# Spreading the softmax reciprocals over the heads' partitions: a matrix product with diagonal blocks, or a trip through memory

## The chip, the cores and the metric

One core of a Trainium2 chip runs the whole layer in one launch. The metric is device time in microseconds; several runs are made and their median is compared. A profiled execution of the same kernel gives the trace that all durations below come from.

## The reference, cut to what matters

Three blocks follow each other on x (4 batches, 256 tokens, width 256): cross-attention to a context of 4096 rows per batch, a layer that sends a quarter of the tokens to self-attention and the rest to a selective scan (ssm), and a mixture of 8 experts of which each token uses 2. The change lies in the cross-attention alone:

```python
q1 = split_heads(x1 @ Wq1, N1)                     # 8 heads of 64
k = jnp.concatenate([k1, k2], axis=1)              # 256 own keys and 4096 context keys
v = jnp.concatenate([v1, v2], axis=1)
sim = jnp.einsum('bihd,bjhd->bhij', q1, k) * scale
attn = jax.nn.softmax(sim, axis=-1)
out = jnp.einsum('bhij,bjhd->bihd', attn, v)
return out.reshape(B, N1, h * d) @ Wo + bo
```

The kernel divides by the softmax sum after the product with v: each row of `out` is multiplied with the reciprocal of its sum of exponentials.

## The kernel before, in words

**Groups and steps.** The cross-attention takes two heads at a time: 4 batches times 4 pairs are 16 groups, G = 0 to 15. A group has 8 steps s, each of 32 queries against all 4352 keys, so the loop runs over n = 8G + s, and two more steps drain it. In a step `scores(n)` makes the scores in PSUM (su), `copy_max` (L1299) brings them to SBUF and takes maxima, `stat` (L1311, L1316) joins the maxima, `exps` (L1327) makes exponentials and their sums ls for the step before, and `turn` (L1336) transposes them. A step is 128 partitions: 4 quarters of the keys times 32 queries.

**What fills a step.** The rest of TensorE's time in a step goes to `pieces`: at s = 0, 6 and 7 keys of the next group (`k_chunk`, psk, L1226, copied by ACT at L1214), at s = 2, 3 and 4 values of this group (`v_chunk`, psv, L1263, copied at L1267), and at s = 1 and 5 `values(m)`: 136 products po (L1345) that multiply the exponentials of four steps with v. One po holds 64 dimensions of each of two heads on the partitions and 128 queries along the free axis; `values_out` (L1382) copies it to ao.

**The sums.** After a group's last exponentials, at s = 0 of the next group, `sums(G-1)` adds the four quarters' sums with a product (psl, L1359) and takes reciprocals (rl, L1364): they lie as 2 heads x 32 queries on 64 partitions, 8 steps along the free axis. The normalisation wants them the other way: queries along the free axis, the same value on all 64 partitions of a head. Before, DVE multiplies rl with diagonal blocks (dg, 64 x 256, L1366), and at s = 1, between the first and second piece of po, `spread` multiplies dg with a constant of ones per head (pair) on TensorE: psr, 128 x 256, in PSUM (L1373). `normalize` (L1388) multiplies ao with it, one half in the middle of step s = 1 and one at its end.

**Queues, banks and order.** The order of all instructions is written out by hand (`manual_schedule`). Side work (router, small attention, ssm scan of the batch before) is made of generators that `slot` lets run one piece at a time, by a planned time `now` to which each piece adds its cost. Three PSUM banks with the tag "m" (`bank`, and the tiles psk, psv, po) serve all of these in turn; a tile waits until the earlier tile in its bank has been read. In-order engines: what waits, holds back all behind it. The SP queue issues nearly all loads: the context chunks ctx (512 KB each, `load_ctx`, L1130; four buffers, so that SP runs ahead by four), weights, and in the scans bb and cb (L615), spread copies of the ssm's B and C, which POOL uses at L637 and L650. The pieces of side work that are named below run for batches 0, 1 and 2 beside the groups of the next batch (the first of them at G = 4, 8 and 12): pspr (L553), its copy projT (L557), psas (L419), psdt (L579) and its readers delta and ev (L586), psat (L437), pa (L427, L428); at a scan's end zs (L764) and pssd (L769); after the last group psx (L1392) and the experts.

Of the kernel before, what the change touches and what calls it, by code (L numbers as in the profile page):

```python
# [8 lines left out]
F32 = mybir.dt.float32  # L9
AF = mybir.ActivationFunctionType  # L10
ALU = mybir.AluOpType
# [3 lines left out]
P = 128  # L15
B, T, D = 4, 256, 256
# [3 lines left out]
H, HD = 8, 64  # L20
# [17 lines left out]
def bc(ap, axis, n):  # L38

    ap = ap.unsqueeze(axis)  # L40
    shape = list(ap.shape)
    shape[axis] = n
    return ap.to_broadcast(shape)
# [3 lines left out]
def perceiver_layer(ctx: ExitStack, tc: tile.TileContext, a: dict, out: bass.AP):  # L47
    nc = tc.nc
# [5 lines left out]
    dram = ctx.enter_context(tc.tile_pool(name="dram", bufs=2, space=bass.MemoryType.DRAM))  # L54
    fin = ctx.enter_context(tc.tile_pool(name="fin", bufs=1))
# [166 lines left out]
    def bank(name):  # L222
        return ps_m.tile([P, 512], F32, tag="m", name=name)
# [831 lines left out]
    now = [0.0]  # L1055
    active = []

    def start(g):
        active.append([g, now[0], 0.0])
# [6 lines left out]
    def slot(budget):  # L1066

        room[0] = budget
        for item in list(active):
            if item[1] <= now[0] and item[2] <= room[0]:  # L1070
                room[0] -= item[2]
                step(item)

    def step(item):
        r = next(item[0], None)
        if r is None:
            active.remove(item)
        else:
            item[1:] = now[0] + r[0], r[1]
# [23 lines left out]
    with ExitStack() as s1:  # L1103
# [17 lines left out]
        def load_self(G):  # L1121
            return load_weights(G, ("wk1", "wq1"), "wself", 1)
# [26 lines left out]
        def load_later():  # L1149
# [11 lines left out]
        dm = same[:, 0, :]  # L1161
        nc.vector.tensor_reduce(
            out=dm, in_=ident.rearrange("p (c i) -> p i c", c=4), axis=AX.X, op=ALU.add
        )
        for q in range(1, 4):
            nc.vector.tensor_copy(same[:, q, :], dm)
        quarter = fin.tile([P, 4, 2], F32, name="quarter")
        nc.vector.tensor_reduce(
            out=quarter[:, :, 0], in_=ident.rearrange("p (c i) -> p c i", c=4), axis=AX.X,
# [17 lines left out]
        def turn_x(b):  # L1187
# [9 lines left out]

        su = ps_s.tile([P, 5 * 512], F32, name="su")


        pair = fin.tile([2 * 32, P], F32, name="pair")
        nc.vector.tensor_copy(
            pair.rearrange("p (j d) -> p j d", j=2), bc(quarter[: 2 * 32, 0:2, 0], 2, HD)
        )
        qzs = [fin.tile([P, 2, T], F32, name=f"qz{i}") for i in range(2)]
        for t in qzs:
            nc.gpsimd.memset(t, 0.0)
# [11 lines left out]
        def k_chunk(G, g):  # L1219
            b = G // NHP  # L1220
            if G not in kts:
                kts[G] = wk.tile([P, 4, QK], F32, tag="kt", name="kt")
            ct = load_ctx(b, g)
            ps = ps_m.tile([P, 512], F32, tag="m", name="psk")
            for c in range(KD):
                nc.tensor.matmul(  # L1226
                    ps, wqk[G][:, 0, c, :], ct[:, c, :],
                    start=(c == 0), stop=(c == KD - 1),
                )
            keys_out(G, g * (CK // 4), ps)  # L1230
# [118 lines left out]
                        start=(k == 0), stop=(k == NJ - 1),  # L1349
                    )  # L1350

        dgs, rss = {}, {}

        def sums(G):

            b, hp = divmod(G, NHP)
            ps = bank("psl")
            for j in range(2):
                nc.tensor.matmul(  # L1359
                    ps[j * 32 : (j + 1) * 32, :8], dm, lss[b][:, hp, :, j],  # L1360
                    start=True, stop=True,
                )
            rl = fin.tile([2 * 32, 8], F32, tag="rl", name="rl")
            nc.vector.reciprocal(rl, ps[: 2 * 32, :8])  # L1364
            dgs[G] = fin.tile([2 * 32, 8, 32], F32, tag="dg", name="dg")
            nc.vector.tensor_tensor(  # L1366
                dgs[G], bc(rl, 2, 32), bc(dm[: 2 * 32, :], 1, 8), ALU.mult
            )

        def spread(G):  # L1370

            rss[G] = bank("psr")[:, :T]
            nc.tensor.matmul(  # L1373
                rss[G], pair, dgs[G].rearrange("p s i -> p (s i)"), start=True, stop=True
            )

        def values_out(m):
# [39 lines left out]
        with tc.manual_schedule():  # L1417
            norms = {}
            k_chunk(0, 0)
            wself[0] = load_self(0)  # L1420
            nc.scalar.dma_start(out=bo_bc, in_=a["xbo"].partition_broadcast(P))
            for _ in norm(0):
                pass
            for g in range(1, NCH):
                k_chunk(0, g)
                if g == 4:
                    turn_x(0)
            k_self(0)
            start(load_later())
            wv[0] = load_v(0)  # L1430
            N = 8 * NG
            for n in range(N + 2):
                G, s = divmod(n, 8)
                new, old = n < N, 1 <= n <= N


                pieces, took = [], 1.75
                if s == 5 and G + 1 < NG:
                    wv[G + 1] = load_v(G + 1)
                if s % 4 == 1:  # L1440
                    m, took = n // 4 - 1, 1.95
                    if m >= 0:
                        pieces = [
                            lambda i=i: values(m, i, min(i + 9, NJ)) for i in range(0, NJ, 9)
                        ]
                elif 2 <= s <= 4 and G < NG:
                    pieces = [
                        lambda g=g: v_chunk(G, g) for g in range(3 * s - 6, 3 * s - 3)
                    ]
                elif G + 1 < NG:  # L1450
                    if s == 0:
                        wqk[G + 1] = load_qk(G + 1)
                        wself[G + 1] = load_self(G + 1)
                    pieces = {
                        0: [lambda g=g: k_chunk(G + 1, g) for g in range(3)],
                        6: [lambda g=g: k_chunk(G + 1, g) for g in range(3, 6)],
                        7: [lambda: k_self(G + 1)]
                        + [lambda g=g: k_chunk(G + 1, g) for g in range(6, 8)],
                    }[s]


                tail = n >= N - 2

                def piece(i):
                    if i < len(pieces):
                        pieces[i]()
                    if i < len(pieces) or tail:
                        now[0] += took

                if new:  # L1470
                    scores(n)
                    now[0] += 2.1
                if old:
                    exps(n - 1)
                if new:
                    copy_max(n)
                piece(0)
                if s % 4 != 1:
                    slot(1.3)
                    piece(1)  # L1480
                    if old:
                        turn(n - 1, 0)
                    if new:
                        stat(n)
                        now[0] += 0.3
                    if s == 0 and n:
                        sums(G - 1)
                        now[0] += 0.2
                    if old:
                        turn(n - 1, 1)  # L1490
                    slot(1.3 if tail else 0.5)
                    piece(2)
                    slot(2.9)
                else:
                    last = s == 1 and G
                    if last:
                        spread(G - 1)
                        now[0] += 0.6
                    slot(1.5)
                    piece(1)  # L1500
                    if new:
                        stat(n)
                        now[0] += 0.3
                    slot(2.8)
                    if last:
                        normalize(m - 1)
                    if n == N + 1:

                        psx[B - 1] = bank("psx")
                        project(B - 1, 0, psx[B - 1], range(NHP))  # L1510
                        add(B - 1, 0, psx[B - 1])
                        project(B - 1, 1, psx[B - 1], range(NHP - 1))
                    piece(2)
                    slot(1.5)
                    piece(3)
                    if n > 4:
                        values_out(m)
                    if old:
                        turn(n - 1, 0)
                        turn(n - 1, 1)  # L1520
                    if last:
                        normalize(m)
                        if m % 8 == 7:
                            start_first(finish_batch(m // 8))
                b = n // 32 + 1
                if b < B:
                    if n % 32 == 20:
                        norms[b] = norm(b)
                    if n % 32 in (20, 22):
                        next(norms[b])  # L1530
                    if n % 32 == 29:
                        turn_x(b)
# [299 lines left out]
```

## Time and profile before

| | |
|---|---|
| median of 3 runs | 1555.44 us (1549.75 to 1558.04) |
| profiled execution | 1555.58 us, of which the span 1553.9 us |
| mean granted TensorE clock | 0.977 |
| TensorE (PE) busy | 1461.9 us, 94% |
| VectorE (DVE) busy | 1057.1 us, 68% |
| ScalarE (ACT) busy | 758.9 us, 49% |
| GpSimd (POOL) busy | 412.0 us, 27% |
| DMA | 223.41 MB, 144 GB/s mean |
| psr: 32 passes (16 products) | 376 to 793 ns each |
| dg: 16 instructions | 416 to 757 ns each |

The span is the time from the first to the last instruction in the profile. A line of the timeline has the start in us, the length in us of a run of like instructions, the engine (SPq and ACTq are DMA issues), the source line, the operation, what it writes and reads, shapes, how many, and in brackets the idle time of the engine before it with what ended that. PEld is the loading of weights, beside PE. Each matrix product in f32 stands as two passes.

### The profile page before, as it was taken

To read this page: it belongs to the slowest core of one execution; us is meant where nothing else is said; L and a number is where in the kernel's file an instruction comes from. 1 tells how busy PE (TensorE), PEld (TensorE's weight loads), DVE (VectorE), ACT (ScalarE), POOL (GpSimd) and SP (SyncE) were. 2 spreads that over 40 slices of the span, in tenths; PEclk is the share of its full clock that TensorE was granted. 3 is DMA by queue.
4 is the path that set the end of the run, shared out by engine and by line. 5 is a ranking of instruction groups with operands and counts; after the bars stand their busy time and mean duration, and the time that the engine had idled before them with its cause. 6 is when DMAs were issued, how large, how long until landed. Compare 5 with 4: busy or idle time off the path is not lost.

```text
span 1553.9 us, 37283 instructions
## 1 busy us (share of the span) xinstructions
PE 1461.9 (94%) x15686; PEld 1039.5 (67%) x15686; DVE 1057.1 (68%) x1812; ACT 758.9 (49%) x1486; POOL 412.0 (27%) x464
## 2 busy tenths in 40 slices
PE   7999999999999999999999999999998868988799
PEld 3757667576667475766665767757665558778587
DVE  1666666666699976565999866658988633499453
ACT  3444454454666644555667454546664413534211
POOL 1000000000089940000799500005996011110100
PEclk9999999999999999999999999999999968999899
DMA  7445543524344525243454343334543115777471
GB/s 240 149 131 160 161 139 107 180 72 143 120 147 140 182 83 192 79 145 100 141 176 158 113 144 126 99 112 162 159 127 114 42 55 183 253 250 259 125 233 48
DMA packets 157767, 223.41 MB, mean 144 GB/s; under 512 B 14976, under 2 KB 76160, under 8 KB 157600
## 3 DMA queue, kind: packets, MB, share of 16 engines
q1 hardware_dynamic: 152368, 211.45, 42.7%
q10 hardware_dynamic: 3744, 5.51, 1.1%
q0 software_dynamic: 1488, 4.07, 0.9%
q8 instruction: 124, 2.03, 0.5%
q14 instruction: 43, 0.35, 0.1%
HBM read 216.56 MB, written 4.42 MB: 142 GB/s over the span
## 4 chain that ended last, share of the span: by engine, by line
PE 63%; POOL 14%; DVE 13%; issue 4%; ACT 3%; DMA 2%; ACTq 0%; SPq 0%; DVEq 0%; POOLq 0%
PE po L1345 12%; PE su L1279 11%; PE psv L1263 11%; PE psk L1226 9%; POOL y L652 5%; POOL db L637 5%; POOL db L650 4%; DVE sp L1299 4%; PE su L1287 2%; PE pg L1749 2%; PE pu L1749 2%; PE pde L1762 2%; DVE pt L1336 2%; DVE db L739 1%; DVE db L644 1%
## 5 line engine op out<-in xcount | busy, mean ns | idle before, releaser
L1299 DVE TENSOR_SCALAR_CACHE_REDUCE sp<-su 128x1088 f32<-128x1088 f32 x256 | 318.8, 1281 | 182.0 <-PE su L1287 182.0
L1336 DVE STREAM_TRANSPOSE pt<-sp 128x1088 f32<-128x1088 f32 x256 | 328.0, 1295 | 57.0 <-PE po L1345 56.9
L1327 ACT ACTIVATE sp<-sp,nb 128x1088 f32<-128x1088 f32 x256 | 305.2, 1195 | 13.9 <-DVE nb L1316 13.7
L1345 PE MATMUL po<-pt,v 128*64 128x128 f32 x4352 | 263.9, 278 | 2.3 <-DVE pt L1336 1.3
L1279 PE MATMUL su<-kt,qz 64*32 64x512 f32 x4096 | 256.0, 609 | 4.4 <-DVE nb L1316 3.7
L1226 PE MATMUL psk<-ctx,wk 128*128 128x512 f32 x512 | 245.1, 612 | 10.2 <-DMA ctx<-in_ctxT 7.7
L1345 PEld LDWEIGHTS po<-pt,v 128*64 128x64 f32 x4352 | 241.7, 139 | 14.1 <-issue 7.7
L1263 PE MATMUL psv<-wv,ctx 128*128 128x128 f32 x2048 | 250.3, 279 | 0.6 <-DMA ctx<-in_ctxT 0.3
L1263 PEld LDWEIGHTS psv<-wv,ctx 128*128 128x128 f32 x2048 | 236.1, 192 | 6.7 <-issue 1.4
L1226 PEld LDWEIGHTS psk<-ctx,wk 128*128 128x128 f32 x512 | 91.4, 191 | 94.3 <-issue 85.0
L1214 ACT COPY kt<-psk 128x512 f32<-128x512 f32 x128 | 74.8, 585 | 158.6 <-PE psk L1226 158.4
L1279 PEld LDWEIGHTS su<-kt,qz 64*32 64x32 f32 x4096 | 63.3, 108 | 124.4 <-issue 93.0
L652 POOL TENSOR_TENSOR y<-y,db 128x192 f32<-128x192 f32 x192 | 135.2, 704 | 15.1
L1267 ACT COPY v<-psv 128x512 f32<-128x512 f32 x144 | 79.2, 558 | 119.8 <-PE psv L1263 118.5
L644 DVE TENSOR_TENSOR_SCAN db<-da,db 128x384 f32<-128x384 f32 x96 | 123.2, 1284 | 14.4 <-POOL db L637 3.7
L650 POOL TENSOR_TENSOR db<-db,cb 128x384 f32<-128x384 f32 x96 | 110.8, 1154 | 26.4 <-DVE da L642 26.4
L395 POOL TENSOR_TENSOR kbd<-qk,hmask 128x512 f32<-128x512 f32 x8 | 8.2, 1045 | 407.1 <-ACT qk L385 407.1
L637 POOL TENSOR_TENSOR db<-bb,xc 128x384 f32<-128x384 f32 x96 | 111.2, 1181 | 0.2
L1287 PEld LDWEIGHTS su<-kt,qz 128*32 128x32 f32 x2048 | 34.6, 109 | 109.3 <-issue 109.3
L632 ACT ACTIVATE da<-delta,A_log_sb 128x192 f32<-128x192 f32 x192 | 75.4, 447 | 51.1 <-DVE da L642 38.4
L1382 ACT COPY ao<-po 128x128 f32<-128x128 f32 x32 | 8.5, 264 | 152.5 <-PE po L1345 152.5
L1311 PEld LDWEIGHTS su<-mq,same 128*128 128x128 f32 x256 | 41.1, 191 | 54.7 <-DVE mq L1306 37.8
(278 smaller groups left out, 1587.2 us busy)
## 6 DMA issues: line engine op xcount, KB each, us to landing
ctx<-in_ctxT SPq DMA_DIRECT2D x256, 512.0 KB, 4.8
gateT<-in_gateT SPq DMA_DIRECT2D x27, 512.0 KB, 4.0
upT<-in_upT SPq DMA_DIRECT2D x27, 512.0 KB, 5.1
downT<-in_downT SPq DMA_DIRECT2D x27, 512.0 KB, 6.2
bb<-bcd SPq DMA_DIRECT2D x24, 192.0 KB, 4.3
cb<-bcd SPq DMA_DIRECT2D x24, 192.0 KB, 3.6
wv<-in_wv SPq DMA_DIRECT2D x32, 128.0 KB, 2.4
in_w<-in_in_w SPq DMA_DIRECT2D x32, 128.0 KB, 3.8
```

What stands on the lines that cost most here:

```text
L637: nc.gpsimd.tensor_tensor(db, bbs[k], bc(xc[:, m, :], 1, SG), ALU.mult)
L644: nc.vector.tensor_tensor_scan(out=db, data0=da, data1=db, initial=0.0, op0=ALU.mult, op1=ALU.add,)
L650: nc.gpsimd.tensor_tensor(db, db, cbs[k], ALU.mult)
L652: nc.gpsimd.tensor_tensor(y[:, m, :], y[:, m, :], db[:, s, :], ALU.add)
L1226: nc.tensor.matmul(ps, wqk[G][:, 0, c, :], ct[:, c, :], start=(c == 0), stop=(c == KD - 1),)
L1263: nc.tensor.matmul(ps[:, i * P : (i + 1) * P], lhsT, wv[G][:, w, c, :], start=(c == 0), stop=(c == KD - 1),)
L1267: nc.scalar.copy(v.rearrange("p k d -> p (k d)"), ps[:, : n * P])
L1279: nc.tensor.matmul(su[q * 32 : (q + 1) * 32, SC[j] + lo : SC[j] + lo + 512], qT[r, j, s * 32 : (s + 1) * 32], kt[r, q, lo : lo + 512], sta ...
L1299: nc.vector.tensor_scalar(out=sps[n][j], in0=su[:, SU[j] : SU[j] + QK], scalar1=1.0, scalar2=None, op0=ALU.mult, op1=ALU.max, accum_out=nm ...
L1327: nc.scalar.activation(sps[n][j], sps[n][j], AF.Exp, bias=nbs[n][:, j : j + 1], accum_out=lss[b][:, hp, s, j : j + 1],)
L1336: nc.vector.transpose(pts[m, j][:, i, :], sps[n][j])
L1345: nc.tensor.matmul(pos[m][j * HD : (j + 1) * HD, :], vts[m // 2, k // 4][:, k % 4, j * HD : (j + 1) * HD], pts[m, j][:, :, kk * 32 : (kk + ...
```

## The change

The diagonal blocks, the constant of ones and the product go. `spread` now lies at s = 0, right after the third piece and before the last `slot`, and holds three DMAs: two on ACT's queue, one for each head, that write the 32 x 8 reciprocals into memory with queries contiguous, and one on SP's queue that reads each head's 256 values into all of its 64 partitions (rs in SBUF, 128 x 256). `normalize` reads rs. The 0.6 us that the plan added for the product is gone too.

```diff
-        pair = fin.tile([2 * 32, P], F32, name="pair")
-        nc.vector.tensor_copy(
-            pair.rearrange("p (j d) -> p j d", j=2), bc(quarter[: 2 * 32, 0:2, 0], 2, HD)
-        )
...
-        dgs, rss = {}, {}
+        rls, rss = {}, {}
...
-            rl = fin.tile([2 * 32, 8], F32, tag="rl", name="rl")
-            nc.vector.reciprocal(rl, ps[: 2 * 32, :8])
-            dgs[G] = fin.tile([2 * 32, 8, 32], F32, tag="dg", name="dg")
-            nc.vector.tensor_tensor(
-                dgs[G], bc(rl, 2, 32), bc(dm[: 2 * 32, :], 1, 8), ALU.mult
-            )
+            rls[G] = fin.tile([2 * 32, 8], F32, tag="rl", name="rl")
+            nc.vector.reciprocal(rls[G], ps[: 2 * 32, :8])
 
         def spread(G):
 
-            rss[G] = bank("psr")[:, :T]
-            nc.tensor.matmul(
-                rss[G], pair, dgs[G].rearrange("p s i -> p (s i)"), start=True, stop=True
+            rd = dram.tile([2, 8, 32], F32, tag="rd", name="rd")
+            for j in range(2):
+                nc.scalar.dma_start(
+                    out=rd[j].rearrange("s i -> i s"), in_=rls[G][j * 32 : (j + 1) * 32, :]
+                )
+            rss[G] = fin.tile([P, T], F32, tag="rs", name="rs")
+            nc.sync.dma_start(
+                out=rss[G],
+                in_=rd.rearrange("j s i -> j (s i)").unsqueeze(1).to_broadcast([2, HD, T]),
             )
...
                     slot(1.3 if tail else 0.5)
                     piece(2)
+                    if s == 0 and n:
+                        spread(G - 1)
                     slot(2.9)
                 else:
                     last = s == 1 and G
-                    if last:
-                        spread(G - 1)
-                        now[0] += 0.6
                     slot(1.5)
```

## The prediction

> **What bounds the kernel now.** I read the page first: engine shares, slices, chain.
>
> ```profile
> PE 1461.9 (94%) x15686; PEld 1039.5 (67%) x15686; DVE 1057.1 (68%) x1812; ACT 758.9 (49%) x1486; POOL 412.0 (27%) x464
> ...
> PE po L1345 12%; PE su L1279 11%; PE psv L1263 11%; PE psk L1226 9%; POOL y L652 5%; POOL db L637 5%; POOL db L650 4%; DVE sp L1299 4%; PE su L1287 2%; PE pg L1749 2%; PE pu L1749 2%; PE pde L1762 2%; DVE pt L1336 2%; DVE db L739 1%; DVE db L644 1%
> ```
>
> TensorE carries the attention stage; in three stretches (about 440-555, 765-870 and 1075-1190 us) the chain runs through POOL and DVE, the selective scan. Next the busy time by stretch: one without side work, one inside a scan.
>
> ```profile
> 228.00:262.00 34.00, 34.00 (x433) 22.89 (x432) 20.72 (x35) 14.50 (x26) 0.00 (x0) 1.00 0.50 157
> ...
> 780.00:805.00 25.00, 25.00 (x324) 17.46 (x317) 24.27 (x39) 15.34 (x32) 22.77 (x26) 1.00 0.47 121
> ```
>
> The columns are length, PE, PEld, DVE, ACT, POOL, clock, DMA share, GB/s. Without side work PE has no gap, so what leaves PE shortens the kernel; in a scan DVE and POOL are full. Then the timeline around one product with the diagonal blocks (G=0):
>
> ```profile
> 98.00 0.45 SPq L1130 DMA_DIRECT2D ctx<-in_ctxT  x1
> ...
> 99.09 0.20 DVE L1364 RECIPROCAL rl<-psl 64x8 f32<-64x8 f32 x1
> 99.33 0.42 DVE L1366 TENSOR_TENSOR dg<-rl,same 64x256 f32<-64x256 f32 x1
> ...
> 103.10 2.19 PE L1345 MATMUL po<-pt,v 128*64 128x128 f32 x36
> ...
> 105.22 0.70 PE L1373 MATMUL psr<-dg,pair 64*128 64x256 f32 x2
> ...
> 105.84 2.19 PE L1345 MATMUL po<-pt,v 128*64 128x128 f32 x36
> ...
> 108.47 0.28 DVE L1388 TENSOR_TENSOR ao<-ao,psr 128x128 f32<-128x128 f32 x1
> ```
>
> Nine microseconds lie between the reciprocal and its first use, and DVE's next instruction starts only at 112.09: that is the room for a trip through memory. Last, PE's timeline for G=4, where side work shares the three PSUM banks:
>
> ```profile
> 399.06 1.08 PE L419 MATMUL psas<-kbd,qk 128*64 128x512 f32 x4 [0.49 <-ACT projT L557]
> ...
> 407.67 0.66 PE L437 MATMUL psat<-ident,pa 128*128 128x128 f32 x4 [1.45 <-ACT ev L586]
> ```
>
> psas does not read projT and psat does not read ev: PE waits for a bank to be emptied, while psr holds another.
>
> **What the Trainium skill says.** (1) "DMA: Bandwidth & Descriptors", section "Why a DMA increments its semaphore by 16 and not by 1": a DMA runs on the largest k up to 16 that divides the outermost sizes of both sides. The new read's source is [2, 64 repeats, 256], so k=2; no DMA of before shows that. (2) The same page, "Rules for kernel authors": a last dimension that isn't contiguous becomes one descriptor per element. The trace agrees: behind the 512-element column load dt_b lies a burst of 544 packets, nearly all of 4 bytes (9 ns each), in 1.1 us. (3) The same page, "Two DMAs through the same engine are not ordered": the issuer must wait for the first DMA's semaphore; in the built program the read on SP waits for both writes. (4) "Perfetto Trace Analysis", "Optimization Strategy": consistent bubbles can mean too little PSUM; the 0.49 and 1.45 us above, there at G=4, 8 and 12, agree.
>
> **Removed, PE.** In the 64 po matmuls that start at 108.28 and take 3.71 us they follow each other every (3.71-0.28)/63 = 0.0545 us. From 103.10 to 105.84 are 2.74 us; 36 matmuls need 1.96; so a psr pair with its two changes of shape takes 0.78. At G=0 to 3, 7 and 11 PE has no other limit: 6 x 0.78 = 4.7 us. At G=4, 8, 12 psr is followed by pspr, where one change of shape (0.2, the step into psr) remains: 3 x 0.58 = 1.7. At G=15 PE runs at half clock (1.50 us from the po before to the po after, less a step of 0.1) and the tail waits for it: 1.4.
>
> **Removed, a PSUM bank.** Comparing the two built programs with their waits: instructions keep their order on every engine, only the psr, dg and pair instructions are gone; psat now waits for the first psdt's ev, two reads earlier, psas for a kt copy that is long done, psdt for pa. So 0.49+1.45 = 1.94 us go at each of G=4, 8, 12: 5.8 us. What is late next is psat's own input pa, done by 402.3, ahead of 405. The planner's lost 0.6 us per group moves nothing.
>
> **Removed, DVE.** Sixteen dg of 0.42 us; beside free DVE time they are worth nothing. At G=5, 9, 13 dg takes 0.76 and is in the chain: 3 x 0.7 = 2.1 us. The normalising product reads SBUF instead of PSUM: 32 x 0.25, between 0.1 less and 0.1 more each, 0 taken, since it lies in idle DVE time.
>
> **Added: the trip.** Per group two issues on ACT, one on SP. ACT: 0.34-0.48 us per issue in the trace, so 0.9 us ahead of the next exps (or da); those feed transposes over 6 us later (101.45 to 112.09): nothing. At G=14 ACT reaches the issue 2.75 us before the reciprocal (1171.95, 1174.70), with the da's of a scan behind it that starts at 1182.5: nothing. The issues stand behind the last kt copy, which ends 2.3 us after the reciprocal (1.8 in scan stretches). Writes of 256 4-byte elements: lower end 1.4 us (bcd, 24 KB out to memory), upper end 6.9 (a column load behind other traffic); I take 2.0, as the queue on ACT is empty. The second lands 4.75 us after the reciprocal. SP then issues the read: first packet 1.0 us later (bcd: 0.85), 64 packets of 1 KB on each of two engines at 46 ns (median of such packets) = 2.95, 0.6 to report: 4.5 us. Lower end 2.4 (wv, the same 128 KB on all engines); upper end 8.6, with 110 ns per packet, near the 104 mean of the broadcast bb and cb. rs is there 9.3 us after the reciprocal; DVE can wait until 12.4 without side work (11.8 at G=6, 10, 14): hidden, with 2.5 to 3.1 to spare.
>
> **Added: SP waits, and what is queued behind.** SP holds the read from its turn until the writes land, and in order behind it stand four ctx loads (at G=2 they were issued at 229.4, 233.5, 235.3 and 237.5) that now start about 241. On the two engines the first ctx follows the read: 5.75+2.95 = 8.7, plus 16 packets of 2 KB at 84 ns = 1.35, plus 0.6 = 10.7 us after the reciprocal. The first psv needs it at 14.9 less 0.8 = 14.1: 3.4 spare (2.5 at G=5, 9, 13, where cb and bb stand between). Hidden, but at G=0, where constants stand between (5.3 us of issues in before), I charge 1.0. At G=6 and 10 a cb load (531.44) now starts at about 546.5 and lands at 551.5, while the product that needs it (L650) starts at 549.62 and POOL is the chain: 2 us late, half of it regained because POOL then runs beside less DVE work; the saved 0.8 is lost and 0.6 more: -1.2 for both. At G=14 the delayed cb lands about when it is needed (1182.35): +0.5 kept.
> Tail, G=15: no copy ahead on ACT; rs at 1255.55+0.9+1.8+4.5 = 1262.8, psx needs it at 1265: hidden.
>
> **Sum.** 4.7+1.7+1.4+5.8+2.1+0.5-1.2-1.0 = 14.0 us. The profiled execution took 1555.58 us (span 1553.9, 1.7 around it), 0.1 from the runs' median of 1555.44: 1541.5 us.
>
> **Rivals.** (A) Forecast: gain 8 to 20 us. (B) The gain is swallowed: PE's savings before a scan's end are lost where zs waits for POOL, and bank waits are replaced by psat's or psdt's data. For it: about a third of the chain near the scans is POOL and DVE; against: G=4 has no other late input. Without the 5.8 and with cb 3 us late twice: 14-5.8-4 = 4, 1551. (C) Slower: the SP hold. If writes take 3.6 us (the quickest column loads of 1 KB and more) and the read 8.6, the chain is 5.7 late; the first psv then waits 5.7-3.1 = 2.6 us on average at 13 groups, 34 us against 14 gained: 1575. It decides from about 3 us over my estimate and costs 13 us per us beyond; at 4.1 over it cancels the gain. For it: nothing in before shows two-engine reads or 4-byte writes to memory; against: packet costs are measured and both rings are empty then. (D) The freed bank removes further waits in psv and the trip is quicker than thought: gain over 20, about 1532.
>
> **Chances.** A 0.60, B 0.17, C 0.14, D 0.09. Half a per cent is 7.8 us, about what a measurement here tells from no change. Faster: A, D and 0.02 of B = 0.71; same 0.15; slower 0.14. The range leaves out C's most (above) and D's better half: 1534 to 1557.
>
> **What would show it.** po groups 1.96 us apart with nothing between; psas and psat without waits; rs landing in 4 to 5 us from issue, ahead of ao; ctx issued in a burst some 5 us after rl; psv without a wait on DMA ctx; POOL L650 idle on cb about 2 us at two groups. Wrong if psv or ao wait for DMAs at most groups, or if rs takes over 8 us.

## The result, and the profile after

The changed kernel takes 1591.83 us (median of 4 runs, 1589.5 to 1593.62) where the kernel before took 1555.76 on the same chip: ratio 1.0239, 95% interval 1.0222 to 1.0256. It is 36 us slower; the forecast was 14 us faster. The span of its profiled execution is 1591.8 us, the mean granted clock 0.971.

The page after, engines and chain, as the first two lines of before were read:

```profile
PE 1465.2 (92%) x15654; PEld 1046.4 (66%) x15654; DVE 1054.1 (66%) x1795; ACT 759.7 (48%) x1486; POOL 397.5 (25%) x464
...
PE su L1274 9%; PE psk L1221 9%; PE psv L1258 9%; PE po L1340 8%; DVE sp L1294 5%; POOL y L652 4%; POOL db L650 4%; DVE db L644 3%; POOL db L637 3%; DVE pt L1331 2%; DMA rs<-rd 2%; DMA rd<-rl 2%; DMA ctx<-in_ctxT 2%; PE pg L1747 2%; PE su L1282 2%
```

TensorE's share fell from 94% to 92% although the product is gone, and three DMAs stand in the chain that were not there: the write of the reciprocals (rd<-rl), the read (rs<-rd), and the context loads. A stretch without side work, 34 us long as in the prediction (columns: stretch, length, PE, PEld, DVE, ACT, POOL, clock, DMA share, GB/s):

```profile
232.00:266.00 34.00, 31.81 (x383) 20.93 (x376) 19.84 (x33) 14.86 (x27) 2.30 (x3) 1.00 0.42 137
```

PE had no gap in such a stretch before; now it stands for 2.2 us at full clock. The timeline around the first trip (G=0; start, length, engine, line, operation, shapes, and in brackets the idle time before it with what ended that) shows where:

```profile
98.26 0.20 DVE L1359 RECIPROCAL rl<-psl 64x8 f32<-64x8 f32 x1
...
100.20 0.85 ACTq L1367 DMA_DIRECT2D rd<-rl  x2
102.27 4.15 PE L1340 MATMUL po<-pt,v 128*64 128x128 f32 x72
...
106.83 3.71 PE L1340 MATMUL po<-pt,v 128*64 128x128 f32 x64
...
107.28 0.66 SPq L1371 DMA_DIRECT2D rs<-rd  x1
...
111.36 0.73 SPq L1130 DMA_DIRECT2D ctx<-in_ctxT  x1
...
112.20 0.29 DVE L1387 TENSOR_TENSOR ao<-ao,rs 128x128 f32<-128x128 f32 x1 [5.10 <-DMA rs<-rd]
...
115.66 2.66 PE L1258 MATMUL psv<-wv,ctx 128*128 128x128 f32 x12 [2.88 <-DMA ctx<-in_ctxT]
```

The writes are issued at 100.20 and SP, which waits until both have landed, issues the read at 107.28: 7.1 us, where 2.0 was priced. I call this time the landing. From there two waits follow. DVE stands 5.10 us for rs, and PE stands 2.88 us for a context chunk whose load was queued behind the read. The po runs, in between which the product stood, are gapless, as forecast. Over the whole kernel (waits by engine, line and what was waited for: us in all, times, longest):

```profile
DVE ao L1387 <- DMA rs<-rd: 73.5, 16, 9.7
...
PE psv L1258 <- DMA ctx<-in_ctxT: 28.1, 14, 3.5
...
POOL db L650 <- DMA cb<-bcd: 20.3, 3, 7.3
```

Before, the same view has one wait of psv for context, and none of db for cb:

```profile
PE psv L1263 <- DMA ctx<-in_ctxT: 0.3, 1, 0.3
```

The loads of cb stand behind the read on SP's queue, as those of ctx do; POOL's three waits for them are 7.3, 7.2 and 5.9 us long.

The write's landing is late at all 16 groups: the read goes out 6.5 to 8.1 us after the first write's issue, median 7.1 (6.7 from the second write's). The packets don't tell this: at G=2 the last of 544 packets of 4 bytes, 7 ns each, is on record as done 3.3 us after the reciprocal, and the read goes out 9.0 us after it.

To place the loss I cut the spans at the reciprocals. Interval k runs from the reciprocal of group k-1 to that of group k, and holds the spreading and normalising of group k-1. Differences to before, us, for the changed kernel and for the first experiment, which has no trip:

| interval | 0 | 1-4 | 5, 9, 13 | 6, 10, 14 | 7, 11, 15 | 8, 12 | tail | all |
|---|---|---|---|---|---|---|---|---|
| changed kernel | -0.8 | +13.5 | -12.3 | +10.8 | +20.5 | +3.9 | +2.3 | +37.9 |
| no trip | -0.9 | -3.1 | -12.2 | +4.0 | +1.0 | -1.6 | -4.7 | -17.5 |

The second row is what the removal is worth, the difference of the rows (55.4 us) is what the trip costs. The trip costs nothing at 5, 9 and 13, and 2.6 to 7.6 us at most other intervals; at 7, 11 and 15, where POOL's three waits for cb lie, it costs 7.6, 7.2 and 4.7.

Only part of the 55.4 us is PE standing still. PE idles 126.6 us of the changed kernel's span and 92.5 us without a trip: that is 34.1. For the other 21.3 us it is busy longer with as many products. This line of the kernel without a trip is to be read beside the first one above:

```profile
PE 1443.9 (94%) x15654; PEld 1032.6 (67%) x15654; DVE 1062.2 (69%) x1795; ACT 758.4 (49%) x1486; POOL 403.3 (26%) x465
```

The granted clock accounts for it. The traces list stretches, 3.4 us long or a multiple of that, in which TensorE is granted half its clock: 93.5 us of the changed kernel, 52.6 without a trip. The 40.9 us more are worth some 20 us of work. The mean clock of all runs says the same (0.966 to 0.973 against 0.980 to 0.983). The first wait for context (G=0) and the one at G=2, in the view by stretches:

```profile
112.78:115.66 2.88, 0.00 (x0) 0.03 (x1) 2.88 (x4) 0.48 (x2) 0.00 (x0) 1.00 0.85 223
115.90:119.30 3.40, 3.28 (x16) 2.98 (x15) 2.99 (x6) 0.09 (x1) 0.00 (x0) 0.50 0.95 237
...
259.00:261.00 2.00, 0.12 (x1) 0.15 (x2) 1.60 (x3) 0.44 (x2) 0.00 (x0) 1.00 1.06 395
261.00:275.00 14.00, 13.73 (x148) 11.94 (x148) 11.57 (x18) 5.31 (x9) 0.00 (x0) 1.00 0.62 208
```

After 2.88 us of standing the clock is 0.50 for 3.4 us, after the wait of 1.92 us at G=2 it stays at 1.00; intervals 1 and 2, which have such a stretch each, lose 5.4 and 5.7 us, intervals 3 and 4 without one 2.8 each. That the waits bring the half clock fits this, but no experiment tests it by itself. The kernels differ by such stretches ahead of the first reciprocal too, where no trip has run, so one stretch (1.7 us of loss) more or less in a single interval of a single profile should not be read as an effect of an edit.

### The profile page after: what moved, and what is told of

It is laid out like the page before. It is cut to its first block, busy times and chain, and to the rows that moved or that the text cites. A ratio compares the mean times of both kernels' runs of the same rounds, so it can differ in the third digit from the quotient of the medians.

```text
span 1591.8 us, 37309 instructions
## 1 busy us (share of the span) xinstructions
PE 1465.2 (92%) x15654; PEld 1046.4 (66%) x15654; DVE 1054.1 (66%) x1795; ACT 759.7 (48%) x1486; POOL 397.5 (25%) x464
## 4 chain that ended last, share of the span: by engine, by line
PE 55%; DVE 18%; POOL 11%; DMA 9%; issue 4%; ACT 2%; SPq 0%; ACTq 0%; DVEq 0%; POOLq 0%
PE su L1274 9%; PE psk L1221 9%; PE psv L1258 9%; PE po L1340 8%; DVE sp L1294 5%; POOL y L652 4%; POOL db L650 4%; DVE db L644 3%; POOL db L637 3%; DVE pt L1331 2%; DMA rs<-rd 2%; DMA rd<-rl 2%; DMA ctx<-in_ctxT 2%; PE pg L1747 2%; PE su L1282 2%
## 5 line engine op out<-in xcount | busy, mean ns | idle before, releaser
L1258 PE MATMUL psv<-wv,ctx 128*128 128x128 f32 x2048 | 256.2, 283 | 28.1 <-DMA ctx<-in_ctxT 28.1
L1258 PEld LDWEIGHTS psv<-wv,ctx 128*128 128x128 f32 x2048 | 241.9, 196 | 34.9 <-issue 30.2
L650 POOL TENSOR_TENSOR db<-db,cb 128x384 f32<-128x384 f32 x96 | 106.3, 1107 | 65.5 <-DVE da L642 45.2
L637 POOL TENSOR_TENSOR db<-bb,xc 128x384 f32<-128x384 f32 x96 | 99.3, 1056 | 0.2
```

The source lines that it names most:

```text
L637: nc.gpsimd.tensor_tensor(db, bbs[k], bc(xc[:, m, :], 1, SG), ALU.mult)
L650: nc.gpsimd.tensor_tensor(db, db, cbs[k], ALU.mult)
L1258: nc.tensor.matmul(ps[:, i * P : (i + 1) * P], lhsT, wv[G][:, w, c, :], start=(c == 0), stop=(c == KD - 1),)
```

## The experiments

| kernel | median us | ratio to before, 95% interval | read's issue after the first write's, median us |
|---|---|---|---|
| changed kernel | 1591.83 | 1.0239, 1.0222 to 1.0256 | 7.1 |
| no trip | 1540.32 | 0.9917, 0.9893 to 0.9940 | none |
| late normalising | 1602.91 | 1.0314, 1.0282 to 1.0346 | 7.7 |
| read by ACT | 1613.0 | 1.0382, 1.0355 to 1.0410 | 8.5 |
| both of these | 1570.53 | 1.0121, 1.0093 to 1.0148 | 8.8 |
| rows of 128 bytes | 1540.54 | 0.9915, 0.9886 to 0.9943 | 1.6 |
| pieces of 32 bytes | 1541.67 | 0.9924, 0.9897 to 0.9951 | 1.9 |
| 4 bytes, 512 apart | 1540.64 | 0.9926, 0.9900 to 0.9952 | 2.2 |
| 4 bytes, 64 apart | 1540.41 | 0.9918, 0.9900 to 0.9936 | 2.2 |
| rows, one hop | 1545.72 | 0.9965, 0.9949 to 0.9982 | 3.5 |
| rows, two hops | 1568.44 | 1.0105, 1.0086 to 1.0124 | 5.6 |
| before, bank freed early | 1550.58 | 0.9985, 0.9975 to 0.9995 | none |
| the same, copy in PSUM | 1599.19 | 1.0296, 1.0280 to 1.0311 | none |
| no trip, constant in PSUM | 1589.97 | 1.0234, 1.0209 to 1.0259 | none |
| rows, copy in PSUM | 1594.62 | 1.0261, 1.0246 to 1.0276 | 1.6 |
| rows, second half from its bank | 1539.38 | 0.9913, 0.9900 to 0.9927 | 1.6 |

### Is it the trip at all?

```diff
-            rd = dram.tile([2, 8, 32], F32, tag="rd", name="rd")
...
-                in_=rd.rearrange("j s i -> j (s i)").unsqueeze(1).to_broadcast([2, HD, T]),
-            )
+            rss[G] = fixed
```

> The changed kernel without any of its three DMAs: normalize multiplies with a constant tile, so the division by the softmax sums is left out. What is left of the change is the removal alone. If the terms of the sum for what is removed hold (psr on TensorE, the freed PSUM bank, dg in the scans), 1539 to 1542 us. If removing the product is worth little (its time or the bank waits come back elsewhere), 1550 to 1556. Then the trip costs some 50 us, or some 38.

1540.32 us. The time is the one that the sum forecast (its terms are taken up below); all of the loss is the trip's.

### Which of the two holds costs: SP's queue or DVE?

Normalising moved to the next group's third step (a batch's last group apart, whose projection follows at once), so that DVE no longer stands:

```diff
+                    if s == 2 and G and not late_ok(G):
+                        normalize(2 * G - 2)
+                        normalize(2 * G - 1)
...
-                    if last:
+                    if last and late_ok(G):
```

> The changed kernel with both normalizing products of a group moved from step s=1 to the end of step s=2 (but for a batch's last group), so that VectorE no longer waits for rs ahead of its transposes; SP's hold stays. If the loss of step s=2 comes from VectorE held by rs: 1555 to 1565 us. If it comes from the ctx loads that stand behind the read on SP: 1580 to 1590.

The read moved to ACT's queue in step s = 1, so that SP's loads no longer stand behind it:

```diff
-            nc.sync.dma_start(
+            nc.scalar.dma_start(
...
+                    if last:
+                        fetch(G - 1)
```

> The changed kernel with the read of rs issued by ACT, in step s=1 at the old place of the product, so that SP's ctx loads aren't held by the writes; VectorE waits for rs as before. If the ctx loads behind SP's hold make the loss: 1555 to 1566 us, and psv without a wait for ctx. If VectorE's wait for rs makes it: 1583 to 1592.

Neither came out cheaper than the change itself: 1602.91 and 1613.0. In the first, with SP's hold alone (but for the batch ends), PE waits for context as long as without the edit (31.5 us against 28.1):

```profile
PE psv L1258 <- DMA ctx<-in_ctxT: 31.5, 12, 4.8
```

In the second PE waits for no context chunk in psv, but DVE stands at rs, and PE's stat products stand for mq, which DVE then makes late (23.7 us in 21 waits without a trip):

```profile
DVE ao L1392 <- DMA rs<-rd: 85.0, 16, 10.2
...
PE su L1306 <- DVE mq L1301: 62.4, 24, 7.4
```

This kernel is not DVE's hold alone: ACT, which now issues the read, stands for the landing too (15.5 us ahead of da, 6.9 ahead of projT); those waits lie in stretches with side work. In intervals 1 to 3, where there is none, the loss against the kernel without a trip is 5.9, 5.2 and 4.8 us with SP's hold alone, 6.7, 4.3 and 4.9 with DVE's, and 5.4, 5.7 and 2.8 with both. The holds lie side by side, so each suffices and removing one gains nothing. In the second, the landing is also later (8.5 us), beside context loads that are no longer held back. So I took both away, with the 4-byte pieces left as they are:

> The write stays as the change has it, in 4-byte pieces; but the normalisation of each group waits until the end of the next group's scan (a batch's last group apart), and the read back is issued by ACT at the scan's first step, so that neither SP's queue nor DVE stands at the write's landing. Two holds theory (held SP and held DVE are the whole loss): no wait of PE on ctx above 3 us, DVE's wait on rs below 2 us each away from the batch ends, 1541 to 1555 us. Rival (the 256 small packets of each write, or ACT's two issues of 0.3 to 0.8 us, hurt by themselves): 1575 us or more, with the loss still in the scans' second steps.

1570.53: between the two forecasts, and the intervals say why. In 1 to 3, where both holds are off, the kernel equals the one without a trip to 0.0, -0.1 and 0.0 us, although the landing is the latest of all (8.8). So the hold that each single edit left in place is what cost there. The loss stands where the edit couldn't reach: at the batch ends (G = 3, 7, 11, 15) DVE still waits, 6.9, 6.3, 6.2 and 10.0 us, and intervals 4, 8, 12 and the tail lose 6.1, 2.6, 4.2 and 6.0 (6.8, 0 and 3.4 us at half clock make the difference between the first three). DVE's waits for rs are just these four:

```profile
DVE ao L1392 <- DMA rs<-rd: 29.4, 4, 10.0
```

At intervals 9 and 13, which lose 3.6 and 3.7 us, a hold of the edit's own is at work: ACT stands 6.6 and 6.9 us for the landing with projT behind it, and each has one stretch at half clock. The 3.0 us ahead of the first reciprocal, where no trip has run yet, are 6.8 us at half clock, of which the kernel without a trip has none there. The small packets and the issues by themselves cost nothing that intervals 1 to 3 show.

### Why does the write land late?

The reciprocals are first turned on DVE (32 x 32 blocks), so that each head writes 8 rows of 128 contiguous bytes:

```diff
-            nc.vector.reciprocal(rls[G], ps[: 2 * 32, :8])
+            nc.vector.reciprocal(rlp[:, :8], ps[: 2 * 32, :8])
+            rls[G] = fin.tile([2 * 32, 32], F32, tag="rl", name="rl")
+            nc.vector.transpose(rls[G], rlp)
...
-                    out=rd[j].rearrange("s i -> i s"), in_=rls[G][j * 32 : (j + 1) * 32, :]
+                    out=rd[j], in_=rls[G][j * 32 : j * 32 + 8, :]
```

> The changed kernel with the reciprocals transposed on VectorE first (32x32 blocks), so that each head's write is 8 rows of 128 contiguous bytes in place of 256 separate 4-byte elements. If the slow landing (about 7 us from issue) is that of scattered 4-byte writes: landing in 2 to 3 us, rs there some 4 us earlier, 1543 to 1556 us. If any write to memory takes that long to be reported: 1588 to 1592, landing as before.

1540.54 us: the whole loss is gone with the trip still there. Its timeline at G=2:

```profile
235.13 0.20 DVE L1360 RECIPROCAL rlp<-psl 64x8 f32<-64x8 f32 x1
235.37 0.20 DVE L1362 STREAM_TRANSPOSE rl<-rlp 64x32 f32<-64x32 f32 x1
...
237.07 0.62 ACTq L1370 DMA_DIRECT2D rd<-rl  x2
...
238.70 0.52 SPq L1374 DMA_DIRECT2D rs<-rd  x1
...
244.66 0.29 DVE L1390 TENSOR_TENSOR ao<-ao,rs 128x128 f32<-128x128 f32 x1 [0.85 <-DMA rs<-rd]
```

The read goes out 1.6 us after the writes, and DVE waits 0.85 us where it waited 5.7 in the change. Rows differ from the change in the size of a piece, in their number, and in whether neighbours in memory are written apart. Three kernels separate these; each leaves out a part of the work. 32 rows of 32 bytes a head, without the tokens' order:

```diff
-                    out=rd[j].rearrange("s i -> i s"), in_=rls[G][j * 32 : (j + 1) * 32, :]
+                    out=rd[j], in_=rls[G][j * 32 : (j + 1) * 32, :]
```

> Each head's 32 x 8 reciprocals are written as 32 pieces of 32 contiguous bytes, straight from rl, in the order in which they lie; the order by tokens is left out, so that the normalisation uses the reciprocals of other tokens. Theory that the number of 4-byte pieces makes the landing late (256 a head): 32 pieces land in 2 to 3 us from the first issue instead of 6.9, and the time is 1540 to 1550 us. Rival (any write of the reciprocals by pieces far below a line, or the receipt of any write, lands late): 5 us or more from the issue, 1575 to 1595 us.

Then 256 pieces of 4 bytes again, but no two near each other:

```diff
-            rd = dram.tile([2, 8, 32], F32, tag="rd", name="rd")
+            rd = dram.tile([2, 8, 32, 128], F32, tag="rd", name="rd")
...
-                    out=rd[j].rearrange("s i -> i s"), in_=rls[G][j * 32 : (j + 1) * 32, :]
+                    out=rd[j, :, :, 0].rearrange("s i -> i s"),
+                    in_=rls[G][j * 32 : (j + 1) * 32, :],
```

> The same 4-byte pieces, 256 a head, each put 512 bytes from its neighbours; read back to a small tile of 16 rows by SP, and the normalisation takes a constant, so that the division by the sums is left out and DVE waits for no transfer. Theory A (pieces that lie side by side in one line wait for each other in memory): landing in 2 to 3 us from the first issue, 1541 to 1550 us. Theory B (256 pieces of 4 bytes are slow wherever they lie): about 7 us from the first issue to the read's issue; SP's hold is then alone, and costs the scans 35 us or more, as where normalising was moved late: 1575 to 1603 us.

And with 16 in place of 128 in the last dimension:

> As the kernel that writes the 4-byte pieces 512 bytes apart (the division by the sums is left out, the normalisation takes a constant), but 64 bytes apart. If pieces wait for each other only within 64 bytes: read issued 2.0 to 2.3 us after the first write's issue as at 512 bytes, 1539 to 1543 us. If the unit is larger (up to 512 bytes, so that 8 pieces share one): 2.5 to 7 us.

The timeline at G=2, with pieces 512 bytes apart:

```profile
236.57 0.81 ACTq L1369 DMA_DIRECT2D rd<-rl  x2
...
238.62 0.55 SPq L1374 DMA_DIRECT2D rs<-rd  x1
```

And 64 bytes apart:

```profile
237.03 0.81 ACTq L1369 DMA_DIRECT2D rd<-rl  x2
...
239.08 0.55 SPq L1374 DMA_DIRECT2D rs<-rd  x1
```

2.05 us both times (median 2.2 over all groups), with as many 4-byte pieces as the change has. So neither their size nor their number by itself makes the landing late. It is that 4-byte pieces lie side by side: in the change all 32 queries of a step fill 128 contiguous bytes, each written by itself, and 7.1 us pass. These two kernels also free DVE from its wait, and one could think that this makes the writes quick; but with both holds off and the pieces side by side the landing took 8.8. Whether the pieces wait for each other in memory or on the way to it these runs don't tell, nor in which unit; pieces 64 bytes apart show nothing of it.

### How late may the trip be?

One more copy from memory to memory on SP between the write and the read of the kernel with rows, and then two:

```diff
+            rd1 = dram.tile([2, 8, 32], F32, tag="rd1", name="rd1")
+            nc.sync.dma_start(out=rd1, in_=rd)
+            rd = rd1
```

> The kernel with rows of 128 bytes, and one more trip from memory to memory by SP between write and read. The hop adds about 2 us, so that the read is issued some 4 us after the first write's issue, 2 us over the forecast's estimate. By the forecast's slack (3 us) nothing is lost at SP, and DVE waits 1 to 3 us more in some groups: 1540 to 1546 us. Rival (no slack, each us late costs 13): 1560 us or more.

> The same with two more trips: the read is issued some 6 us after the first write's issue, 4 us over the estimate, about 1 us short of the change's own. By the forecast's slack the scores' second steps lose in most groups, 13 us and DVE's share on top: 1556 to 1580 us. Rival (it is not the lateness but the many small packets that cost): 1540 to 1548 us.

The read's issue, as a median after the reciprocals are ready (turned, where they are turned), and the time: 3.1 us and 1540.5; 5.0 and 1545.7; 7.0 and 1568.4; the change itself, 8.5 and 1591.8. The slope is 11 us per us from 5.0 to 7.0 and 16 from 7.0 to 8.5. The two-hop kernel has few packets, in rows of 128 bytes, and loses through the same waits, so lateness by itself makes a loss:

```profile
DVE ao L1396 <- DMA rs<-rd: 47.8, 14, 7.3
...
PE psv L1260 <- DMA ctx<-in_ctxT: 16.2, 10, 2.3
```

### Where does the freed bank's gain go?

The kernel before, with its product, and only the bank freed early by a copy on ACT:

```diff
-            rss[G] = bank("psr")[:, :T]
+            ps = bank("psr")[:, :T]
...
+            rss[G] = fin.tile([P, T], F32, tag="rs", name="rs")
+            nc.scalar.copy(rss[G], ps)
```

> The kernel before, with its product, and one added copy by ACT of the product's result from its PSUM bank to SBUF, right after the product, from where DVE normalises: the bank is free earlier, all else stays, and ACT has 0.3 to 0.5 us more per group. If the bank's term of the forecast (5.8 us over G4, G8 and G12) comes through to the end: 1548 to 1551 us. If it is swallowed ahead of the next scan: 1553 to 1557 us.

1550.58 us, 3.1 less than before. By interval it gains 2.3, 3.8 and 2.2 us at 5, 9 and 13 (the bank's own term was 1.9 each; at 9 and 13 a stretch at half clock in before is part of the difference) and loses 3.2 and 3.1 at 6 and 10, where it has a stretch at half clock each that before hasn't (1.7 us), and 0.7, 0.6 and 1.7 at 7, 11 and 15; without the tail's 4.5, to which I come below, it would be slower than before. The step in which interval 6 loses first is read best on two engines at once, before the copy and with it. Before:

```profile
480.10 1.66 POOL L650 TENSOR_TENSOR db<-db,cb 128x384 f32<-128x384 f32 x1
...
480.87 0.25 DVE L1388 TENSOR_TENSOR ao<-ao,psr 128x128 f32<-128x128 f32 x1
...
486.83 0.30 PE L1311 MATMUL su<-mq,same 128*128 128x8 f32 x2
```

With the copy:

```profile
478.95 1.65 POOL L650 TENSOR_TENSOR db<-db,cb 128x384 f32<-128x384 f32 x1
...
479.73 1.03 DVE L1390 TENSOR_TENSOR ao<-ao,rs 128x128 f32<-128x128 f32 x1
...
487.25 0.39 PE L1311 MATMUL su<-mq,same 128*128 128x8 f32 x2 [1.40 <-DVE mq L1306]
```

The same product beside the same POOL instruction takes 1.03 us in place of 0.25, and ends just after POOL's (480.76 and 480.60). Its second operand moved from PSUM to SBUF. The Trainium skill says this ("SBUF — State Buffer", section "Who interferes with whom"): a DVE instruction with two SBUF inputs contends with a GpSimd instruction that reads SBUF. The traces agree: all 32 products take 8.36 us before, 15.64 with the copy, 16.21 in the kernel without a trip, and every long one lies in a scan. DVE is nearly full there (24.27 of 25 us in the prediction's stretch), and PE's stat product then waits 1.40 us for mq. To take this away I put the operand back into PSUM, in spare columns of su:

```diff
+    SR = 2 * 512 + 192
...
-            rss[G] = fin.tile([P, T], F32, tag="rs", name="rs")
+            rss[G] = su[:, SR : SR + T]
             nc.scalar.copy(rss[G], ps)
```

> As the kernel that copies psr out of its bank with ACT, but the copy goes to 256 spare columns of su, in PSUM, so that DVE's normalising product has one operand in SBUF as before. Theory (two SBUF operands make the product wait for the POOL instruction beside it, which is what takes the bank's gain back in the scans of G6 and G10): the products take 0.25 to 0.29 us again instead of up to 1.03, the step after the normalisation of G5 and G9 is 8.0 us again instead of 9.4 to 9.7, and the time is 3 to 5 us under that kernel's: 1545 to 1548 us. Rival (the scans swallow the gain whatever the product costs): 1549 to 1553 us.

> As the kernel without transfers, whose normalisation takes a constant (the division by the sums is left out), but the constant stands in spare PSUM columns. Theory of the POOL wait: 3 to 5 us under that kernel, 1535 to 1538 us. Rival: 1539 to 1542 us.

> As the kernel that writes the reciprocals in rows of 128 bytes, with one more ACT copy per group of rs from SBUF to spare PSUM columns ahead of the first normalising product. If the POOL wait is what costs and ACT's wait for rs costs nothing: 1535 to 1539 us. If ACT, standing before its copy until rs lands, delays the key and value copies behind it: 1541 us or more.

All three miss, at 1599.19, 1589.97 and 1594.62 us. The products are short again (8.33, 8.31 and 8.53 us for 32), so that much of the theory stands, but su is also the scores' tile, and the program now makes the next scores wait until DVE has read it. In the kernel with the constant:

```profile
PE su L1277 <- DVE ao L1381: 42.5, 15, 2.9
```

That is 2.8 us at 15 groups, much the same in the other two (41.5 and 45.9 in all), and hides what the shorter products bring in all. Against the kernel without a trip the intervals lose 4.3 to 4.5 us where no scan runs (2.8 of waiting and, behind it, 1.7 for a stretch at half clock), but only 0.9 and 0.7 at 6 and 10. Shorter products would give that, but so would a scan that hides a wait of PE, since POOL and DVE are the limit there; these kernels don't separate the two. Twelve of the 15 waits have a stretch at half clock that begins within 1.2 us of their end. Last, the kernel with rows, whose second half DVE multiplies straight from its own bank, without ACT's copy:

```diff
-            nc.vector.tensor_tensor(ao, ao, rss[G][:, q], ALU.mult)
+            nc.vector.tensor_tensor(ao, pos[m] if half else ao, rss[G][:, q], ALU.mult)
```

> The kernel with rows of 128 bytes, in which DVE multiplies the second half of each group straight from its PSUM bank (no ACT copy of that half): one SBUF operand in place of two, and the bank is held until after two transposes, about 3 us longer. If the POOL wait costs and the bank isn't missed: those 16 products take 0.25 to 0.3 us, and the time is 1 to 3 us less, 1537.5 to 1539.5 us. If the longer hold costs PE more: 1541 us or more.

1539.38 against 1540.54 for rows, measured at different times, with overlapping ranges of the ratio: no difference that can be told in the time. The 16 second products are 0.24 to 0.29 us, and intervals 6, 10 and 14 are 1.0, 0.3 and 0.3 us shorter, less than one stretch at half clock costs. That the second SBUF operand makes the product long is shown, and that PE waits behind one such product; how much of the swallowing it is stays open.

## Why the prediction was wrong, point by point

**The step that failed: "I take 2.0, as the queue on ACT is empty".** The landing was 7.1 us from the first write's issue, 6.7 from the second's. The bounds were written as 1.4 to 6.9, and the upper one was nearly it; the choice of the lower part rested on packet times (9 ns each in the burst cited) and on an empty queue. Both were true and neither decides: with 256 pieces a head that don't lie side by side the 2.0 would have held (2.2 from the first write's issue, 1.8 from the second's). The Trainium skill ("DMA: Bandwidth & Descriptors", section "Anatomy of one DMA — SWDGE (gpsimd) path") puts most of a fixed cost of about 2 us on the receipt of the write from memory, for DMAs that GpSimd issues; these are issued by ACT, where the pieces 64 and 512 bytes apart take about as long, 2.2 us, and the side-by-side ones 5 more. The same page ("Specifications") says that below 512 bytes the engine reads, modifies and writes; the runs show that this is not enough for the delay, since pieces of 4 and of 32 bytes were quick, though it could explain why neighbours wait for each other. That was not shown.

**The read** was also mis-sized, by less: 5.9 us from its issue to DVE's first product in the kernel with rows (238.70 to 244.66), 4.6 to 6.9 in the changed one (median 5.9), against 4.5. At G = 15, where no context loads follow it, it takes 4.4 and 4.6 in the two kernels, as priced for two engines; elsewhere packets of 2 KB are on record in the same time (328 of them at G = 2 of the changed kernel) from the loads issued right behind it, which the sum let follow the read on its two engines. With a landing of 2 us this would have been harmless, as the kernel with rows shows.

**The slack.** "It decides from about 3 us over my estimate" counts landing and read together. The read's issue was put 4.75 us after the reciprocal, so the one-hop kernel is 1.7 us over (0.3 in the landing, 1.4 in the read) and the two-hop kernel 3.7. In the profiled runs the first loses 1.1 us against the kernel with rows at intervals 1 to 14 (4.2 more lie ahead of the first trip and at interval 15), the second 20. So the slack ends somewhere between the two, which leaves the 3 standing without showing it. "13 us per us beyond" came out near, at 11 and 16, but in part by luck: it was priced as standing alone, and PE's idle time makes 13.8 of the 17.5 us between the profiled runs with one hop and two, and 17.5 of the 30.3 from there to the change. The rest is PE busy longer, and half clock behind waits stands nowhere in the prediction: a term at nothing.

**What is queued behind.** The mechanism of rival C is one that happened: PE waits for context at 14 groups, at most 3.5 us each. But C named SP's hold alone. DVE's hold, which the prediction passed with "2.5 to 3.1 to spare", is by itself enough in intervals 1 to 3. Two waits that lie side by side are to be priced both: removing one brings nothing. The wait of POOL for cb, priced at 2 us in two groups, was 7.3 and 7.2 there and 5.9 in a third. The tail, "hidden", has DVE's longest wait for rs (9.7 us) and costs 7.0 against the kernel without a trip.

**The range.** The bounds of the write and the read together were in the text (6.9 and 8.6), rival C used 3.6 and 8.6, and the time range ended at 1557 because C was given 14 in 100. With nothing in the profile that showed a 4-byte write into memory, that chance had no ground.

**The removal.** The sum of 14.0 us includes 1.7 of charges for the trip, so the removal alone was forecast at 15.7. Measured are 14.0 in the medians without a trip (1554.31 to 1540.32) and 17.5 in the profiled spans. That this is near is in part luck, for its terms did not all come out:

- The product off PE: 0.78 each forecast, 0.75 to 0.78 measured at intervals 1 to 4, 8 and 12: right.
- The bank at G=4, 8, 12 with the rest of psr: 2.5 each forecast, 3.0, 4.6 and 4.6 measured at intervals 5, 9 and 13; in the last two before has a stretch at half clock, 1.7 us, that the kernel without a trip hasn't. The timeline of the changed kernel shows psas and psat without their waits, as forecast:

```profile
410.03 0.64 PE L419 MATMUL psas<-kbd,qk 128*64 128x512 f32 x1
410.35 1.02 PE L419 MATMUL psas<-kbd,qk 128*64 128x512 f32 x3
...
417.38 0.66 PE L437 MATMUL psat<-ident,pa 128*128 128x128 f32 x4
```

- Inside the scans: 2.1 of gain for dg forecast; measured are 2.9 and 2.2 us of loss at intervals 6 and 10, 1.0 of gain at 14, and 0.1 to 0.5 of loss at 7, 11 and 15. That is rival B's outcome, for 5.0 us. A term of the sum, "0 taken, since it lies in idle DVE time", was wrong: the normalising product with two SBUF operands costs up to 0.78 us more where POOL runs, and DVE has hardly any idle time there. How much of the 5.0 us this makes, beside the waits that B named and a stretch at half clock at interval 6, is open.
- The tail: 1.4 forecast, 4.7 measured, and hardly any of it can be the product's: the two kernels that free the bank early and keep the product gain 4.5 and 4.8 there. Much of it is PE's clock. The windows of before over the last products (same columns as above):

```profile
1255.40:1260.00 4.60, 3.42 (x28) 3.02 (x30) 3.10 (x12) 0.00 (x0) 0.00 (x0) 0.50 0.02 4
1260.00:1266.40 6.40, 6.40 (x51) 5.19 (x47) 0.29 (x1) 0.00 (x0) 0.00 (x0) 0.51 0.00 0
```

and of the kernel with the copy:

```profile
1257.00:1261.50 4.50, 3.20 (x26) 2.80 (x28) 3.22 (x12) 0.00 (x0) 0.00 (x0) 0.50 0.01 4
1261.50:1265.50 4.00, 4.00 (x52) 3.38 (x48) 0.29 (x1) 0.37 (x1) 0.00 (x0) 0.87 0.00 0
```

The clock is 0.50 in both at first; before, it stays near there for 6.4 us more, and the last 36 po products take 4.00 us against 2.19. Whether the early bank brings this or chance, one profile of each can't say; the mean clock of the runs of before lies between 0.975 and 0.982, and the profiled one has 0.977.

**A cost at nothing that held**: ACT's two issues, 0.8 us ahead of its next work, with which the kernel with rows loses nothing against the one without a trip.

## What to carry to other kernels

Price a write to memory by how its pieces lie, not by packets and queue alone: a write that scatters neighbouring 4-byte elements needs its own row in a trace before it may stand ahead of anything, and turning the data on chip first (0.2 us here) makes the trip cost nothing that can be told here (1540.54 against 1540.32 us). For each wait that a DMA brings, list the queue it is issued from and the engine that reads it, and size both against the later landing: taking one away shows nothing while the other remains. Compare PE's idle time and its granted clock as well as the span: a wait of some 3 us can cost half as much again in slower products. When an operand changes its memory, ask which neighbour shares the way to the new one.

## What the runs showed of the hardware that was not expected

- Two writes of 256 4-byte pieces each, side by side in 1 KB each: 7.1 us from the issue to the release of the reader (6.5 to 8.1 at 16 groups); the same pieces 64 or 512 bytes apart: median 2.2; 32 pieces of 32 bytes a head, side by side: 1.9; 8 rows of 128 bytes a head: 1.6. The packets' own record ends some 5.7 us before the release in the first case (3.3 and 9.0 us after the reciprocal at G=2).
- With context loads that are not held back, the same scattered writes land later still: 8.5 and 8.8 us in the median, up to 12.8.
- A DVE product 128 x 128 in f32 takes 0.25 us with one operand in PSUM and up to 1.03 with both in SBUF, beside a POOL product that had begun.
- Behind a wait of TensorE of about 2.8 us there is often a stretch of 3.4 us at half its clock: in the kernel with the constant in PSUM at 12 of 15 such waits, in the kernel before with its copy in PSUM at 8 of 15. Behind the waits of 1.92 and 2.01 us at G=2 and 3 of the changed kernel there is none.
- One more copy of 2 KB from memory to memory, between two DMAs that wait for each other, adds 1.9 to 2.1 us.
